# A graph layer on one core: first gathers taken from x, table B made before table A, lists and attributes loaded in pieces

## The chip, the core and the metric

The kernel runs on one core of a Trainium2 chip. Its engines work from queues of their own and meet through semaphores: TensorE (PE, with its weight loads shown apart as PEld), VectorE (DVE), ScalarE (ACT), GpSimd (POOL) and SyncE (SP), which here only issues transfers. The metric is the device time of one execution in microseconds, the median of several.

## The reference

A message-passing layer on a graph with N = 6250 nodes of H = 128 features and E = 100000 edges with 4 attributes each, all in float32. `dst` is sorted, `src` is not.

```python
msg_in = concatenate([x[src], x[dst], edge_attr], axis=1)      # E x 260
h = silu(msg_in @ mW1 + mb1)
messages = h @ mW2 + mb2
aggregated = segment_sum(messages, dst, num_segments=N)
u = silu(concatenate([x, aggregated], axis=1) @ uW1 + ub1)
updated = u @ uW2 + ub2
out = layernorm(x + layer_norm(x + updated, ln_g, ln_b))
```

## The kernel before, in words

Rather than multiply 260 features for each edge, the kernel first makes two tables of nodes in DRAM: `tab_a = x @ mW1[:128]` and `tab_b = x @ mW1[128:256] + mb1`. An edge's hidden row is then `tab_a[src] + tab_b[dst]` and the product of its four attributes, and after that the silu.

**Prologue.** `x` comes into `x_sb` (49 tiles of 128 nodes) by seven transfers, four on SP and three on ACT. Tiles go in groups of four: PE transposes them (L189), DVE copies the result to `xT` (L190), PE multiplies by the first part of `w1` (L196), ACT copies the product to `ta` (L198), SP stores it to `tab_a` (L199). When all of A is done the same `xT` is multiplied by the second part (L209), DVE adds the bias into `tb` (L211, three buffers) and SP stores it to `tab_b` (L212). Then come the four attribute rows of `mv` (L236); the attributes, which were loaded as one tile `ea_l` (L147), are turned on ACT in one copy (L242) and stored as four long rows `ea_d` (L243); and the lists of edges: `by_lane` (L123, and L128 for the last short group) brings `src_i` and `dst_i` so that a partition holds eight edges of each group, first for 14 groups, later for the other 84. `relative` (L223) forms the offset of each edge's `dst` from its group's first node, and L253 to L261 test that no group spans more than 96 nodes, for which a general path stands at the end. Last come the weights of the node update.

**Edges.** 98 groups of 1024 edges. For group g:

- `fetch` (L281): eight indirect transfers on POOL, each with 128 rows of `tab_a` by `src_i`, into a row buffer `ga`. There are seven buffers (AHEAD + 3).
- `load` (SP): 96 rows of `tab_b` from the group's first node into `mv` (L328), the attribute rows into `st` (L329), and `dst` of the group, broadcast to 96 partitions, into `near` (L334). It stands two groups ahead of the group that uses it.
- `matrices` (DVE): two one-hot matrices, `st` (node by edge, L341, from `near`) and `oh` (edge by node, L349, from `rel`).
- `hidden`: PE multiplies `st` by `mv` (L361, eight matmuls of two instructions each), which gives the B part and the attribute part at once; DVE adds the gathered rows into `s` (L363), after which the row buffer is free; ACT takes the silu into `h` (L365).
- `by_nodes`: PE multiplies `oh` by `h` (L372), ACT copies the sum to `sw` (L374).
- `add`: PE transposes `sw` (L379, L380) and DVE adds it to columns of `acc` and `deg` in SBUF (L383), at an address that is read from `base_i`.

The pools give `near`, `oh`, `s` and `sw` three buffers each, and PSUM two each for `pre`, `pw` and `pt`. SP's queue has the order of the code. On the other engines the scheduler of the language sets the order of work of neighbouring groups.

**Update.** In 13 groups of four tiles and then seven of seven, `acc` is multiplied by `mW2`, the update network is run, and the two layer norms are taken; the output goes out by SP.

Of the kernel before, what the change touches and what calls it, by code (L numbers as in the profile page):

```python
# [8 lines left out]
F32 = mybir.dt.float32  # L9
I32 = mybir.dt.int32  # L10
# [14 lines left out]
def kernel(  # L25
# [53 lines left out]
    LEAD = 2  # L79
    FIRST = 14  # L80
    XC = 8
    NM = 4
    assert NG % RB == 0
# [11 lines left out]


    prologue = ExitStack()
    prologue.enter_context(tc.manual_schedule(engines={ENG.SP}))
    x_sb = consts.tile([P, NT, H], F32, name="x_sb")
    nf = N // P  # L100
    w1 = consts.tile([P, 2, H], F32, name="w1")
    nc.scalar.dma_start(w1, mW1[: 2 * H].rearrange("(s k) f -> k s f", k=P))
    if N % P:
        nc.vector.memset(x_sb[:, nf, :], 0.0)
        nc.sync.dma_start(x_sb[: N - nf * P, nf, :], x[nf * P :])
    for k, (i0, n) in enumerate(groups(nf, XC)):
        eng = nc.sync if k % 2 else nc.scalar
        eng.dma_start(
            x_sb[:, i0 : i0 + n, :], x[i0 * P : (i0 + n) * P].rearrange("(i p) c -> p i c", p=P)
        )  # L110
# [21 lines left out]
    if rest:  # L132
        nc.vector.memset(src_i[:, full, :], 0)
        nc.vector.memset(dst_i[:, full, :], N)
    by_lane(src_i, src, 0, FIRST)
# [3 lines left out]
    by_lane(dst_i, dst, 0, FIRST)  # L139
    attrs = ExitStack()  # L140
    EQ = 80
    EJ = E // EQ
    assert E % EQ == 0
    ea_l = attrs.enter_context(tc.tile_pool(name="attrs", bufs=1, side="right")).tile(
        [EQ, EJ * ED], F32, name="ea_l"
    )
    nc.sync.dma_start(ea_l, edge_attr.rearrange("(q j) d -> q (j d)", q=EQ))  # L147
# [19 lines left out]
    nc.gpsimd.memset(acc, 0.0)  # L167
    deg = consts.tile([1, NW], F32, name="deg")
    nc.gpsimd.memset(deg, 0.0)
# [4 lines left out]
    ea_d = dram.tile([ED, NG * GE], F32, name="ea_d")  # L174
    xT = consts.tile([P, NP], F32, name="xT")
# [7 lines left out]
    with tc.tile_pool(name="tables", bufs=3) as work, tc.tile_pool(  # L183
        name="tables_ps", bufs=2, space=PSUM
    ) as ps:
        for i0, n in groups(NT, 4):
            pt = ps.tile([P, 4, P], F32, name="pt")
            for i in range(n):
                nc.tensor.transpose(pt[:, i, :], x_sb[:, i0 + i, :], ident)  # L189
            nc.vector.tensor_copy(  # L190
                xT[:, i0 * P : (i0 + n) * P], pt[:, :n, :].rearrange("p i f -> p (i f)")
            )
            pa = ps.tile([P, 4, H], F32, name="pa")
            for i in range(n):
                cols = slice((i0 + i) * P, (i0 + i + 1) * P)
                nc.tensor.matmul(pa[:, i, :], xT[:, cols], w1[:, 0, :], start=True, stop=True)  # L196
            ta = work.tile([P, 4, H], F32, name="ta")
            nc.scalar.copy(ta[:, :n], pa[:, :n])  # L198
            nc.sync.dma_start(by_node(tab_a)[:, i0 : i0 + n, :], ta[:, :n])  # L199

        b1 = bcast("b1", mb1)
        zeros = work.tile([W, H], F32, name="zeros")
        nc.vector.memset(zeros, 0.0)
        nc.sync.dma_start(tab_b[NP:NW], zeros)
        for i0, n in groups(NT, 4):
            pb = ps.tile([P, 4, H], F32, name="pa")
            for i in range(n):
                cols = slice((i0 + i) * P, (i0 + i + 1) * P)
                nc.tensor.matmul(pb[:, i, :], xT[:, cols], w1[:, 1, :], start=True, stop=True)  # L209
            tb = work.tile([P, 4, H], F32, name="tb")  # L210
            nc.vector.tensor_add(tb[:, :n], pb[:, :n], b1[:, None, :].to_broadcast([P, n, H]))  # L211
            nc.sync.dma_start(by_node(tab_b)[:, i0 : i0 + n, :], tb[:, :n])  # L212


        base_f = work.tile([1, NG], F32, name="base_f")
        nc.vector.tensor_copy(base_f, base_i)
        p_b = ps.tile([P, NG], F32, name="p_b")
        nc.tensor.matmul(p_b, ones[0:1, :], base_f, start=True, stop=True)
        nc.vector.tensor_copy(base_b, p_b)
        nc.vector.tensor_scalar(base_p, base_b, p_col, None, op0=OP.add)  # L220

# [8 lines left out]
    relative(0, FIRST)  # L230


    mv = []
    for k in range(NM):
        t = consts.tile([K1, H], F32, name=f"mv{k}")
        nc.sync.dma_start(t[W:], mW1[2 * H :])  # L236
        mv.append(t)
    with tc.tile_pool(name="lists", bufs=1) as work, tc.tile_pool(
        name="lists_ps", bufs=1, space=PSUM
    ) as ps:  # L240
        ea_t = work.tile([EQ, ED, EJ], F32, name="ea_t")
        nc.scalar.copy(ea_t, ea_l.rearrange("q (j d) -> q d j", d=ED))  # L242
        nc.sync.dma_start(ea_d[:, :E].rearrange("d (q j) -> q d j", q=EQ), ea_t)  # L243
        if E < NG * GE:
            pad = work.tile([ED, NG * GE - E], F32, name="pad")
            nc.vector.memset(pad, 0.0)
            nc.sync.dma_start(ea_d[:, E:], pad)
        by_lane(src_i, src, FIRST, NG)
        by_lane(dst_i, dst, FIRST, NG)
        relative(FIRST, NG)  # L250
        mid = (W - 1) / 2
        off = work.tile([P, NG, G], F32, name="off")
        nc.vector.tensor_scalar(off, rel, -mid, None, op0=OP.add)  # L253
        nc.vector.tensor_mul(off, off, off)
        far = work.tile([P, 1], F32, name="far")
        nc.vector.tensor_reduce(far, off.rearrange("p g i -> p (g i)"), AX.X, OP.max)
        pf = ps.tile([1, P], F32, name="pf")
        nc.tensor.transpose(pf, far, ident)  # L258
        farthest = work.tile([1, 1], F32, name="farthest")
        nc.vector.tensor_reduce(farthest, pf, AX.X, OP.max)  # L260
        nc.vector.tensor_scalar(bad_i, farthest, mid * mid, None, op0=OP.is_gt)  # L261
    attrs.close()
# [3 lines left out]
    nc.sync.dma_start(w2, mW2)  # L266
    u1 = consts.tile([P, 2, H], F32, name="u1")
    nc.sync.dma_start(u1, uW1.rearrange("(s k) f -> k s f", k=P))
    u2 = consts.tile([P, H], F32, name="u2")
    nc.sync.dma_start(u2, uW2)  # L270
    mb2_row = consts.tile([1, H], F32, name="mb2_row")
    nc.sync.dma_start(mb2_row, mb2.rearrange("(o f) -> o f", o=1))
    ub1_col = consts.tile([P, 1], F32, name="ub1_col")
    nc.sync.dma_start(ub1_col, ub1.rearrange("(f o) -> f o", o=1))
    ub2_b = bcast("ub2_b", ub2)
    g_b = bcast("g_b", ln_g)
    b_b = bcast("b_b", ln_b)
    prologue.close()

    def gather(t, tab, idx):  # L280
        nc.gpsimd.indirect_dma_start(  # L281
            out=t,
            out_offset=None,
            in_=tab[:, :],
            in_offset=bass.IndirectOffsetOnAxis(ap=idx, axis=0),
        )


    with ExitStack() as edges:
        held = edges.enter_context(tc.tile_pool(name="held", bufs=1))  # L290
        gath = edges.enter_context(tc.tile_pool(name="gath", bufs=AHEAD + 3))
# [14 lines left out]
        def fetch(g):  # L306
            if g >= NG:
                return
# [334 lines left out]
```

## Time and profile before

| | |
|---|---|
| median of 3 timed runs | 1445.85 us (1443.38 to 1451.78) |
| profiled execution | 1460.16 us, span 1458.3 us |
| busy share: PE, PEld, DVE, ACT, POOL | 56%, 50%, 27%, 14%, 58% |
| granted TensorE clock, mean over the span | 0.681 |
| DMA, mean over the span | 79 GB/s |

Times in the rows are in us from the start of the span. A timeline row gives start, length, engine, line, operation, what it writes and reads, how many instructions were merged (x), and in brackets the idle time of the engine just before and what ended it. "issue" there means that the profile shows nothing the engine waited for. A row of waits gives the total, the number and the longest. A row of stretches gives, for one stretch of time, the busy us and instruction counts of each engine, then the granted TensorE clock, the share of time in which the DMA engines were busy, and what they moved in GB/s.

### The profile page before, as it was taken

How to read it: one execution, taken by the hardware profiler on the slowest of the kernel's cores; microseconds unless marked ns; L12 is line 12 of the kernel's file. 1: busy time of each engine (PE TensorE's matmuls, PEld its weight loads, DVE VectorE, ACT ScalarE, POOL GpSimd, SP SyncE). 2: the span in 40 equal slices, each digit the busy share in tenths (PEclk: the TensorE clock that was granted, in tenths of full speed). 3: DMA queues.
4: the chain of work that ended last, by engine and by line, in shares of the span. 5: the costliest groups of instructions: out<-in, count | busy, mean ns of one | idle time of the engine just before them, and what ended most of it. 6: DMA issues, size and time to landing. Idle time of an engine off the chain costs nothing.

```text
span 1458.3 us, 11699 instructions
## 1 busy us (share of the span) xinstructions
PE 816.6 (56%) x3782; PEld 727.7 (50%) x3782; DVE 400.1 (27%) x803; ACT 197.9 (14%) x340; POOL 838.8 (58%) x814
## 2 busy tenths in 40 slices
PE   5410565837564673765726726756576647699700
PEld 5300455727453572655716726745465636594300
DVE  2101331313221231222303303323122212344543
ACT  1002110101110110111101101101011101112254
POOL 3670267657666766766667667666766666604110
PEclk9655566757656775667757757757665666689955
DMA  8424532323232332322323323322322222300011
GB/s 203 121 67 88 103 84 79 100 67 98 83 86 67 87 100 58 95 80 82 91 58 96 89 60 96 89 68 84 87 76 80 82 72 82 90 5 0 2 50 39
DMA packets 100906, 114.63 MB, mean 79 GB/s; under 512 B 42245, under 2 KB 78094, under 8 KB 100758
## 3 DMA queue, kind: packets, MB, share of 16 engines
q1 hardware_dynamic: 72358, 60.68, 14.8%
q0 software_dynamic: 25088, 51.43, 13.8%
q10 hardware_dynamic: 3392, 1.70, 0.5%
q8 instruction: 32, 0.52, 0.1%
q14 instruction: 36, 0.29, 0.1%
HBM read 102.47 MB, written 11.28 MB: 78 GB/s over the span
## 4 chain that ended last, share of the span: by engine, by line
PE 48%; issue 26%; another core or an unknown queue 14%; DVE 4%; ACT 4%; SPq 2%; DMA 1%; POOL 1%; DVEq 0%; ACTq 0%
PE pre L361 23%; PE pw L372 17%; ACT o L490 1%; ACT z L475 1%; SPq L128 1%; PE pa L196 1%; PE ps_y L437 1%; PE ps_a L423 1%; DVE s L363 1%; PE ps_u L427 1%; PE pt L380 1%; DVE st L416 1%; PE ps_u L428 1%; PE ps_a L422 1%
## 5 line engine op out<-in xcount | busy, mean ns | idle before, releaser
L281 POOL DMA_INDIRECT ga<-tab_a,src_i x784 | 797.1, 1017 | 464.9 <-issue 227.4
L361 PE MATMUL pre<-mv,st 100*128 100x128 f32 x1568 | 417.6, 415 | 145.2 <-issue 139.1
L361 PEld LDWEIGHTS pre<-mv,st 100*128 100x128 f32 x1568 | 392.5, 333 | 158.4 <-issue 157.3
L372 PE MATMUL pw<-h,oh 128*96 128x129 f32 x1568 | 301.2, 339 | 271.3 <-issue 266.2
L372 PEld LDWEIGHTS pw<-h,oh 128*96 128x96 f32 x1568 | 258.3, 213 | 310.4 <-issue 305.5
L363 DVE TENSOR_TENSOR s<-ga,pre 128x1024 f32<-128x1024 f32 x98 | 119.3, 1217 | 387.9 <-remote 222.1
L349 DVE TENSOR_TENSOR oh<-w_row,rel 128x768 f32<-128x768 f32 x98 | 93.2, 953 | 409.8 <-remote 322.2
L365 ACT ACTIVATE h<-s 128x1024 f32<-128x1024 f32 x98 | 103.7, 1058 | 629.4 <-DVE s L363 455.0
L374 ACT COPY sw<-pw 96x129 f32<-96x129 f32 x98 | 25.0, 255 | 390.6 <-remote 325.4
L341 DVE TENSOR_SCALAR st<-near,base_p 96x1024 f32<-96x1024 int32 x98 | 75.5, 770 | 4.9 <-DMA near<-in_dst_dram 2.7
L439 POOL TENSOR_TENSOR xu<-x_sb,ub_b 128x512 f32<-128x512 f32 (+1 forms) x13 | 15.6, 1204 | 73.1 <-PE pt L380 41.9
L209 PE MATMUL pa<-w,xT 128*128 128x128 f32 x98 | 19.9, 378 | 63.7 <-issue 38.5
L209 PEld LDWEIGHTS pa<-w,xT 128*128 128x128 f32 x98 | 17.9, 280 | 65.4 <-issue 39.3
L471 POOL TENSOR_TENSOR xb<-x_sb,b_b 128x896 f32<-128x896 f32 x7 | 14.5, 2075 | 48.2 <-DVE z L483 48.2
L383 DVE TENSOR_TENSOR acc<-acc,pt 128x96 f32 x98 | 24.2, 247 | 54.1 <-remote 47.1
L380 PE MATMUL pt<-ident,sw 96*1 96x96 f32 x98 | 26.6, 271 | 14.8 <-issue 14.8
L379 PE MATMUL pt<-ident,sw 96*128 96x96 f32 x98 | 27.3, 279 | 11.8 <-issue 11.6
L211 DVE TENSOR_TENSOR tb<-pa,b 128x512 f32<-128x512 f32 (+1 forms) x13 | 8.5, 660 | 75.8 <-remote 67.3
L379 PEld LDWEIGHTS pt<-ident,sw 96*128 96x128 f32 x98 | 16.6, 169 | 13.8 <-issue 13.3
L383 DVE TENSOR_TENSOR deg<-deg,pt 1x96 f32 x98 | 23.1, 235 | 0.6 <-DVE acc L383 0.6
L242 ACT COPY ea_t<-ea_l 80x5000 f32<-80x5000 f32 x1 | 9.0, 8979 | 85.8 <-DMA mv<-in_L_gnn_mW_dram 85.8
L258 PE MATMUL pf<-ident,far 128*1 128x128 f32 x1 | 0.4, 371 | 36.1 <-DMA b_b<-in_L_gnn_ln_b_dram 36.1
(70 smaller groups left out, 318.3 us busy)
## 6 DMA issues: line engine op xcount, KB each, us to landing
near<-in_dst_dram SPq DMA_DIRECT2D x97, 384.0 KB
ga<-tab_a,src_i POOLq DMA_INDIRECT x784
mv<-tab_b SPq DMA_DIRECT2D x98, 48.0 KB
tab_a<-ta SPq DMA_DIRECT2D x12, 256.0 KB
tab_b<-tb SPq DMA_DIRECT2D x12, 256.0 KB
out_dram<-o SPq DMA_DIRECT2D x6, 448.0 KB
st<-ea_d SPq DMA_DIRECT2D x98, 16.0 KB
ea_l<-in_edge_attr_dram SPq DMA_DIRECT2D x1, 1562.5 KB
```

The source lines that it names most:

```text
L209: nc.tensor.matmul(pb[:, i, :], xT[:, cols], w1[:, 1, :], start=True, stop=True)
L281: nc.gpsimd.indirect_dma_start(out=t, out_offset=None, in_=tab[:, :], in_offset=bass.IndirectOffsetOnAxis(ap=idx, axis=0),)
L341: nc.vector.tensor_scalar(stbuf[g % NST][:W], near.pop(g), base_p[:W, g : g + 1], None, op0=OP.is_equal,)
L349: nc.vector.tensor_tensor(oh, w_row[:, None, :].to_broadcast([P, G, W]), rel[:, g, :, None].to_broadcast([P, G, W]), op=OP.is_equal,)
L361: nc.tensor.matmul(pre[:, i, :], st[:, i, :], mv[g % NM], start=True, stop=True)
L363: nc.vector.tensor_add(s, rows.pop(g), pre)
L365: nc.scalar.activation(h[:, :, :H], s, AF.Silu)
L372: nc.tensor.matmul(pw, oh[:, i, :], h[:, i, :], start=i == 0, stop=i == G - 1)
L374: nc.scalar.copy(sw, pw)
L379: nc.tensor.transpose(pt[:, 0, :], sw[:, :H], ident[:W, :W])
L380: nc.tensor.transpose(pt[0:1, 1, :], sw[:, H:], ident[:W, :W])
L383: nc.vector.tensor_add(at, at, of)
```

## The change

- The first five groups (RAW) gather rows of `x` itself, which is an input, instead of rows of `tab_a`. Their product with the first part of `w1` is made in the edge stage: PE transposes the gathered rows into a `pre` buffer, DVE copies them to `xg`, and PE adds their product to the same PSUM tile as that of `st` and `mv`, so that the silu reads PSUM and no `s` is added. The list for these five groups is SP's first transfer, and the gathers are written ahead of the tables. `acc` and `deg` are zeroed on DVE instead of POOL.
- Transposes are followed by table B, and table A is made after it. Both go in groups of eight tiles. `xT` is now copied by ACT; two buffers `t` serve both tables. The PSUM buffers of the edge stage are used for the tables too (`pre` for products, `pt` through `narrow()` for everything small), and its pools are opened at the start.
- Lists come in five parts (5, 9, 28, 28 and 28 groups), the last three in the loop at groups 0, 2 and 4, followed by the comparison and the loads of the update's weights. Attributes come in ten pieces, nine of them in the loop, each eight groups ahead of its use.
- Row buffers go from seven to six (AHEAD + 2); `near`, `oh` and `s` from three to two; `load` brings `near` first.

```diff
+    RAW = 5
     FIRST = 14
-    XC = 8
+    LIST = 28
     NM = 4
...
+    edges = ExitStack()
+    edges.enter_context(tc.manual_schedule(engines={ENG.SP}))
+    held = edges.enter_context(tc.tile_pool(name="held", bufs=1))
+    gath = edges.enter_context(tc.tile_pool(name="gath", bufs=AHEAD + 2))
+    work = edges.enter_context(tc.tile_pool(name="edge", bufs=2))
+    ps = edges.enter_context(tc.tile_pool(name="edge_ps", bufs=2, space=PSUM))
...
+    by_lane(src_i, src, 0, RAW)
+    nc.scalar.dma_start(w1, mW1[: 2 * H].rearrange("(s k) f -> k s f", k=P))
...
-    nc.gpsimd.memset(acc, 0.0)
+    nc.vector.memset(acc, 0.0)
     deg = consts.tile([1, NW], F32, name="deg")
-    nc.gpsimd.memset(deg, 0.0)
+    nc.vector.memset(deg, 0.0)
...
+    def fetch(g):
+        if g >= NG:
+            return
+        rows[g] = gath.tile([P, G, H], F32, name="ga")
+        for i in range(G):
+            nc.gpsimd.indirect_dma_start(
+                out=rows[g][:, i, :],
+                out_offset=None,
+                in_=x if g < RAW else tab_a[:, :],
+                in_offset=bass.IndirectOffsetOnAxis(ap=src_i[:, g, i : i + 1], axis=0),
+            )
+
+    for g in range(RAW):
+        fetch(g)
...
+    def attributes(c):
+        t = turn.tile([EQ, EJ * ED], F32, name="ea_l")
+        chunk = edge_attr[c * EC : (c + 1) * EC]
+        nc.sync.dma_start(t, chunk.rearrange("(q j) d -> q (j d)", q=EQ))
+        ea_l[c] = t
+
+    def attribute_rows(c):
+        t = turn.tile([EQ, ED, EJ], F32, name="ea_t")
+        nc.scalar.copy(t, ea_l.pop(c).rearrange("q (j d) -> q d j", d=ED))
+        rows = ea_d[:, c * EC : (c + 1) * EC]
+        nc.sync.dma_start(rows.rearrange("d (q j) -> q d j", q=EQ), t)
...
+        def product(i0, n, part):
+            pm = ps.tile([P, G, H], F32, name="pre")
             for i in range(n):
                 cols = slice((i0 + i) * P, (i0 + i + 1) * P)
+                nc.tensor.matmul(pm[:, i, :], xT[:, cols], w1[:, part, :], start=True, stop=True)
+            return pm[:, :n]
+
+        for i0, n in groups(NT, G):
+            for k, m in groups(n, 4):
+                pt = narrow()
+                for i in range(m):
+                    nc.tensor.transpose(pt[:, i * P : (i + 1) * P], x_sb[:, i0 + k + i, :], ident)
+                nc.scalar.copy(xT[:, (i0 + k) * P : (i0 + k + m) * P], pt[:, : m * P])
+            pm = product(i0, n, 1)
+            tb = tables.tile([P, G, H], F32, name="t", bufs=2)
+            nc.vector.tensor_add(tb[:, :n], pm, b1[:, None, :].to_broadcast([P, n, H]))
+            nc.sync.dma_start(by_node(tab_b)[:, i0 : i0 + n, :], tb[:, :n])
...
+        attribute_rows(0)
+
+        for i0, n in groups(NT, G):
+            pm = product(i0, n, 0)
+            ta = tables.tile([P, G, H], F32, name="t", bufs=2)
+            nc.scalar.copy(ta[:, :n], pm)
             nc.sync.dma_start(by_node(tab_a)[:, i0 : i0 + n, :], ta[:, :n])
...
+        raw = g < RAW
+        if raw:
+            px = ps.tile([P, G, P], F32, name="pre")
             for i in range(G):
+                nc.tensor.transpose(px[:, i, :], ga[:, i, :], ident)
+            xg = work.tile([P, G, P], F32, name="s")
+            nc.vector.tensor_copy(xg, px)
+        pre = ps.tile([P, G, H], F32, name="pre")
+        st = stbuf[g % NST].rearrange("k (c i) -> k i c", i=G)
+        for i in range(G):
+            nc.tensor.matmul(pre[:, i, :], st[:, i, :], mv[g % NM], start=True, stop=not raw)
+            if raw:
+                nc.tensor.matmul(pre[:, i, :], xg[:, i, :], w1[:, 0, :], start=False, stop=True)
+        if raw:
+            nc.scalar.activation(h[:, :, :H], pre, AF.Silu)
             return h
...
+    for g in range(NG + 2):
+        if g % 2 == 0 and lists:
+            l0, l1 = lists.pop(0)
+            by_lane(src_i, src, l0, l1)
+            by_lane(dst_i, dst, l0, l1)
+            relative(l0, l1)
+            if l1 == NG:
+                compare()
+                weights()
+        for c in range(1, NC):
+            if g == max(1, c * EC // GE - 8):
+                attributes(c)
+            if g == max(1, c * EC // GE - 8) + 1:
+                attribute_rows(c)
+        if g + AHEAD >= RAW:
             fetch(g + AHEAD)
```

What POOL does from its last iota to the node update, before (`acc` and `deg` are the sums, `xu` is the update's):

```order
L157 IOTA p_col_i 128x1
L167 MEMSET acc 128x6368
L169 MEMSET deg 1x6368
L281 DMA ga<-tab_a,src_i 128x128 x784
L439 TENSOR_TENSOR xu<-x_sb,ub_b 128x512 x2
```

and after the change:

```order
L158 IOTA w_row_i 128x96
masks.py:199 AFFINE_SELECT ident<-ident 128x128
L162 IOTA p_col_i 128x1
L190 DMA ga<-in_x_dram,src_i 128x128 x40
L190 DMA ga<-tab_a,src_i 128x128 x744
```

The two memsets are gone, and the first forty of the 784 gathers read `x` and so wait for no table.

PE at the end of the tables and the start of the edges, before (`pa` holds products of either table, `pf` belongs to the comparison, `pre` and `pw` to the edges):

```order
L189 MATMUL pt<-ident,x_sb 128x128
L196 MATMUL pa<-w_63,xT 128x128
L209 MATMUL pa<-w_63,xT 128x128 x49
L258 MATMUL pf<-ident,far 1x128
L361 MATMUL pre<-mv_412,st_485 128x128 x8
L361 MATMUL pre<-mv_414,st_486 128x128 x8
```

and after the change (the row of 50 is the last tile of B and all 49 of A; `s` is here the buffer of `xg`):

```order
L262 MATMUL pt<-ident,x_sb 128x128
L273 MATMUL pt<-base_f,ones 128x98
L255 MATMUL pre<-w_79,xT 128x128 x50
L386 MATMUL pre<-ident,ga 128x128 x8
L392 MATMUL pre<-mv_94,st_449 128x128
L394 MATMUL pre<-w_79,s 128x128
L392 MATMUL pre<-mv_94,st_449 128x128
L394 MATMUL pre<-w_79,s 128x128
```

The comparison's transpose no longer stands between the tables and the edges, and the first group's matmuls are preceded by eight transposes of gathered rows and interleaved with their products.

More of the change, by code (lines that the diff above doesn't have):

```diff
@@ L181, in by_node, with narrow @@
         return t[:NP].rearrange("(i p) f -> p i f", p=P)
[L183 to L193, printed above, removed]
+    def narrow():
+        return ps.tile([P, 4 * P], F32, name="pt")
@@ L198 @@
[L198 to L212, printed above, removed]
@@ L228, in relative @@
         )
[L230 to L250, printed above, removed]
+    relative(0, RAW)
```

307 lines of the change are left out of this document (152 added, 155 removed).

## The prediction

> **What bounds the kernel now.** I read the page first, then the waits, then the timeline of POOL and PE, then stretches of it. From the page, the span, the busy shares and the costliest group:
>
> ```profile
> span 1458.3 us, 11699 instructions
> PE 816.6 (56%) x3782; PEld 727.7 (50%) x3782; DVE 400.1 (27%) x803; ACT 197.9 (14%) x340; POOL 838.8 (58%) x814
> L281 POOL DMA_INDIRECT ga<-tab_a,src_i x784 | 797.1, 1017 | 464.9 <-issue 227.4
> ```
>
> No engine is above 58%. The gathers on POOL are one unbroken list of 784, and their idle time is the thing to explain. The waits split it, and name the other loser:
>
> ```profile
> PEld pw L372 <- issue: 305.5, 208, 4.0
> POOL ga L281 <- issue: 227.4, 746, 0.3
> POOL ga L281 <- DVE s L363: 203.9, 25, 57.9
> ```
>
> The 0.3 us between two gathers belongs to them (0.94 + 0.30 = 1.25 us each, 10 us a group of eight). POOL waits 25 times for `s`, which frees a row buffer. Where in time, from POOL's timeline (start, length, engine, line, what):
>
> ```profile
> 42.24 1.11 POOL L281 DMA_INDIRECT ga<-tab_a,src_i  x1 [30.02 <-DMA tab_b<-zeros]
> 111.06 0.95 POOL L281 DMA_INDIRECT ga<-tab_a,src_i  x1 [0.30 <-issue]
> 169.94 1.21 POOL L281 DMA_INDIRECT ga<-tab_a,src_i  x1 [57.93 <-DVE s L363]
> 1273.32 0.94 POOL L281 DMA_INDIRECT ga<-tab_a,src_i  x1 [0.30 <-issue]
> 1316.16 2.48 POOL L439 TENSOR_TENSOR xu<-x_sb,ub_b 128x512 f32<-128x512 f32 x2 [41.89 <-PE pt L380]
> ```
>
> So the profiled span is four pieces: 42 us before any gather; seven groups gathered and then 58 us of standing still, to 169.9; 91 groups in 169.9 to 1273.3, 12.13 us each; and 185 us from the last gather to the end (43 of them the last edges on PE, the rest the node update). After 169.9 the 24 remaining stalls are 203.9 - 57.9 = 146 us, 6.1 us each and 1.6 us a group; the gathers themselves make 10.5. A run between stalls is 91/25 = 3.64 groups long.
>
> Why POOL stalls although PE is 56% busy is seen in PE's weight loads beside POOL's gathers, in stretches of time (length, then busy us and instructions of PE, PEld, DVE, ACT, POOL, granted clock, DMA share, GB/s), and at the seam between two of them:
>
> ```profile
> 60.00:112.00 52.00, 6.24 (x24) 5.35 (x24) 2.08 (x3) 0.00 (x0) 39.51 (x42) 0.50 0.26 68
> 119.00:123.00 4.00, 2.87 (x10) 2.28 (x10) 2.22 (x4) 0.00 (x0) 0.00 (x0) 0.50 0.31 89
> 185.00:204.00 19.00, 5.52 (x19) 3.23 (x19) 2.03 (x4) 0.26 (x1) 12.06 (x12) 0.54 0.17 45
> 204.00:235.00 31.00, 31.00 (x152) 31.00 (x151) 14.48 (x22) 6.12 (x9) 23.21 (x21) 0.78 0.44 116
> 185.62 0.35 PEld L372 LDWEIGHTS pw<-h,oh 128*96 128x96 f32 x3 [0.45 <-issue]
> 187.75 0.23 PEld L372 LDWEIGHTS pw<-h,oh 128*96 128x96 f32 x1 [1.78 <-issue]
> 199.73 0.94 POOL L281 DMA_INDIRECT ga<-tab_a,src_i  x1 [0.31 <-issue]
> 203.98 3.90 PEld L361 LDWEIGHTS pre<-mv,st 100*128 100x128 f32 x16 [0.64 <-issue]
> 205.68 1.71 POOL L281 DMA_INDIRECT ga<-tab_a,src_i  x1 [5.00 <-DVE s L363]
> ```
>
> PE falls into a crawl: one matmul in 1 to 2 us, waiting for nothing the profile names, while POOL gathers without a break. It starts 15 to 30 us after POOL's restart (169.9, then 185) and ends some 3 us after POOL has run out of buffers and stopped (200.7, then 204). Then PE does five times as much per us, frees a buffer, and POOL starts again. The whole edge stage is this cycle. The same crawl sits in the second half of the prologue, where the B table is made beside the first 56 gathers; it ends at 119, when they are through.
>
> **The change, part by part.** *First gathers.* The raw groups need `src` alone, not table A. Two memsets leave POOL, and the first list is SP's first transfer:
>
> ```profile
> 1.49 5.39 POOL L167 MEMSET acc<- 128x6368 f32 x1
> 6.83 5.39 POOL L169 MEMSET deg<- 1x6368 f32 x1
> 7.32 1.94 PE L189 MATMUL pt<-ident,x_sb 128*128 128x128 f32 x8 [7.32 <-DMA x_sb<-in_x_dram]
> ```
>
> A 512 KB load issued at 1.2 us has landed by 7.3, so a list of 20 KB lands at 3 to 7; take 5. Forty gathers at 1.25 us run from 5 to 55. On DVE the two memsets (at most what they took on POOL, 10.8 us) end by about 15, under the first transposes.
>
> *Tables.* B needs eight transposes and sixteen product instructions per eight tiles, as A did before; A alone needs products. Their pace before:
>
> ```profile
> 27.88 0.91 PEld L189 LDWEIGHTS pt<-ident,x_sb 128*128 128x128 f32 x8
> 31.21 0.91 PEld L189 LDWEIGHTS pt<-ident,x_sb 128*128 128x128 f32 x8
> 19.94 20.03 SPq L199 DMA_DIRECT2D tab_a<-ta  x13
> 44.01 7.66 PE L209 MATMUL pa<-w,xT 128*128 128x128 f32 x40 [3.02 <-DVE tb L211]
> ```
>
> 3.3 us per eight tiles with transposes; 7.66 us per 20 tiles without, 18.8 for all 49; 2.3 us from the last store's issue (39.97) to the first gather (42.24). Without the crawl B would stand at 8 + 20 = 28 and A at 49. But the gathers now run through this stage from 5 on. With the crawl from about 20 (15 us in, the early end; in the prologue of before it came after 9) some three of the six B groups are done; from 20 to 58 PE manages 38/1.7 = 22 of its instructions, one group more; then 2.2 groups x 3.3 = 7, A 17, landing 2.3: table A is there at **84 us** (75 if the crawl starts at 34, 95 if at 9). POOL stands from 55 to 84 and restarts with group 5. Before it restarted with group 7 at 169.9.
>
> *What stood between 119 and 164* goes from the path:
>
> ```profile
> 125.30 8.98 ACT L242 COPY ea_t<-ea_l 80x5000 f32<-80x5000 f32 x1 [85.80 <-DMA mv<-in_L_gnn_mW_dram]
> 136.19 10.46 SPq L128 DMA_DIRECT2D src_i<-in_src_dram  x1
> 147.13 5.24 SPq L128 DMA_DIRECT2D dst_i<-in_dst_dram  x1
> 155.06 0.86 DVE L223 TENSOR_TENSOR rel<-dst_i,base_b 128x672 f32<-128x672 int32 x1 [18.06 <-DMA dst_i<-in_dst_dram]
> ```
>
> The attribute copy (now 0.9 us ten times), the long lists, the comparison and the weights' loads move into the loop. They queue on SP ahead of `near`, `mv` and `st` of a group two ahead, and on ACT ahead of one `h`. I cost them at nothing: a group has 12 us and PE needs 6 of them. If that cover fails, see the last rival.
>
> *Raw groups.* Each adds 8 transposes, a copy of 128x1024 and 16 product instructions on PE, and drops one add. From these rows
>
> ```profile
> 29.43 1.86 PEld L196 LDWEIGHTS pa<-w,xT 128*128 128x128 f32 x16 [0.65 <-ACT ta L198]
> 28.62 1.29 DVE L190 COPY xT<-pt 128x512 f32<-128x512 f32 x2 [2.05 <-PE pt L189]
> 211.11 3.90 PEld L361 LDWEIGHTS pre<-mv,st 100*128 100x128 f32 x16
> 216.90 3.90 PEld L361 LDWEIGHTS pre<-mv,st 100*128 100x128 f32 x16
> ```
>
> an ordinary group takes PE 5.8 us when nothing hinders it; a raw one 5.8 + 0.9 + 1.9 (warm; twice that cold) + 1.3 for the copy it waits on, 10 to 12.7. That is as slow as POOL, so in these five groups the crawl is not caught up from slack: POOL stalls for a whole raw group, about 10 us, twice, where 1.6 a group is in the rate already. I add **10 us** (bounds 0 and 40, the latter five groups each 8 late).
>
> *Rate.* Row buffers go from seven to six, `near`, `oh`, `s` from three to two. While PE is fast it takes a group in 5.8 us and POOL brings one in 10.5, so in 20 us the ring drains by 1.5 groups. A ring of six isn't emptied by that either; run and stall stay. I keep 12.13 us (bounds 11.9 and 12.3). At the end the last backlog is up to one group shorter: 185 becomes 182.
>
> **Sum.** 84 + 93 x 12.13 (1128) + 10 + 182 = **1404 us** of span against 1458.3, 54 less. The profiled execution took 1460.16 us, its span 1458.3; the median of the three timed runs is 1445.85, 0.9% under it. Scaled, 1404 becomes **1392 us**, 3.7% faster. With the bounds of 84, 10 and the rate taken together, 1370 to 1430.
>
> **The rivals.** *No crawl in the tables.* If what slowed PE at 51 to 119 was something else, a cold clock or stores behind gathers, the tables are ready at 49 and POOL runs on from 55: 29 us earlier, 1375 of span, 1363 timed. For it: the clock was 0.50 there. Against it: at 119 to 123 the clock was 0.50 too and ten matmuls took 4 us, with no gather. 0.18. The Trainium skill (TensorE: Matmul & The Clock Gate, Part 1) has the array's clock halve after an idle window of about 3.4 us; by that rule alone PE would lose a factor of two in the tables, and this rival's time would hold. The trace does not bear it out as the cause: the rows of 119 and 60 have the same clock, and 2.5 against 0.5 matmuls per us.
>
> *The shorter ring shortens POOL's runs* (the slower side). If a ring of six takes a whole group off each run, 3.64 becomes 2.6, 93 groups make 36 runs and 35 stalls of 6.1, 213 us where 149 are in the rate: +64, span 1468, timed 1455, 0.7% slower than before. It decides from a run of 2.7 groups down. For it: POOL's stall is nothing but a full ring. Against it: the drain of 1.5 groups above. 0.10.
>
> *The pieces land on the path.* All that was moved into the loop, exposed: lists 16, attributes 9 x 1.1 of SP and 9 x 0.9 of ACT, comparison 4, weights 4: +42, span 1446, timed 1434. Against it: SP runs two groups ahead. 0.10. The Trainium skill (DMA: Bandwidth & Descriptors, Anatomy of one DMA) puts about 2.0 us of fixed cost on every DMA; 24 DMAs more (six for lists, eighteen for attributes) would by that be an estimated 48 us, if none were hidden, and the result 1440. No row here shows such a cost on the path: `near`, `mv` and `st` are three DMAs in each of 98 groups already.
>
> **How the numbers follow.** Forecast 0.62, the rivals 0.18, 0.10, 0.10. From the no-crawl case less its rate bound (1350) to the pieces' case (1440) leaves out the short ring and little more. A measurement of this kernel tells about 0.5% from no change, 7 us: under 1439 is faster. That is the forecast, the first rival and half of the third: 0.85; same, the other half, 0.05; slower 0.10.
>
> **What would show it.** First gather at 3 to 7 us, forty to 55; PE's product instructions slow between about 20 and 58; group 5's gather at 75 to 95; 24 to 27 stalls of about 6 us after it; last gather near 1222. A first `tab_a` gather under 60 is the first rival; 33 stalls or more the second; POOL stalls that end with a late `near` or `ea_t` the third. The forecast is wrong as a whole if the crawl behaves otherwise with six buffers or beside the raw groups.

## The result, and the profile after

The changed kernel takes 1391.15 us (median of 4 runs, 1378.75 to 1396.83) against 1444.62 us for the kernel before (1437.3 to 1451.78): a ratio of 0.9619, 95% interval 0.9535 to 0.9702. The profiled execution took 1396.83 us, its span is 1394.9 us, 63 us shorter than the span before.

From the page of the changed kernel, the span, the busy shares and the two groups of gathers, then from its waits those of POOL and the largest of PE:

```profile
span 1394.9 us, 11854 instructions
PE 834.0 (60%) x3902; PEld 746.2 (53%) x3902; DVE 400.9 (29%) x789; ACT 205.9 (15%) x356; POOL 817.8 (59%) x812
...
L190 POOL DMA_INDIRECT ga<-tab_a,src_i x744 | 748.8, 1006 | 421.3 <-issue 218.0
...
L190 POOL DMA_INDIRECT ga<-in_x_dram,src_i x40 | 38.0, 950 | 14.3 <-issue 11.9
```
```profile
PEld pw L407 <- issue: 236.0, 186, 5.6
POOL ga L190 <- issue: 229.8, 742, 1.6
POOL ga L190 <- DVE s L399: 151.2, 27, 10.7
POOL ga L190 <- DMA tab_a<-t: 42.2, 1, 42.2
```

The 58 us for which POOL stood before is now one wait of 42.2 us for table A, and the other stalls for a row buffer are much as they were: 27 of 5.6 us, where there were 24 of 6.1. Where these lie, from POOL's timeline:

```profile
3.98 1.12 POOL L190 DMA_INDIRECT ga<-in_x_dram,src_i  x1 [2.44 <-DMA src_i<-in_src_dram]
96.06 0.94 POOL L190 DMA_INDIRECT ga<-tab_a,src_i  x1 [42.18 <-DMA tab_a<-t]
1223.02 0.95 POOL L190 DMA_INDIRECT ga<-tab_a,src_i  x1 [0.30 <-issue]
```

So the span is now 96.1 us to group 5's gather, 93 groups in 1127.0 us (12.12 each), and 171.9 us from the last gather's start to the end. Against before, group 5 stands where group 7 stood, 74 us earlier.

What the tables look like beside the raw gathers is seen in the rows of PE's weight loads, DVE and ACT on both sides of one gap, and in stretches of time (the columns as before: PE, PEld, DVE, ACT, POOL, clock, DMA share, GB/s):

```profile
24.88 1.64 PEld L262 LDWEIGHTS pt<-ident,x_sb 128*128 128x128 f32 x8
60.75 3.36 PEld L255 LDWEIGHTS pre<-w,xT 128*128 128x128 f32 x16 [34.23 <-ACT xT L263]
17.75 1.23 DVE L266 TENSOR_TENSOR t<-pre,b 128x1024 f32<-128x1024 f32 x1 [3.03 <-issue]
53.79 1.23 DVE L266 TENSOR_TENSOR t<-pre,b 128x1024 f32<-128x1024 f32 x1 [34.81 <-remote]
60.12 1.07 ACT L263 COPY xT<-pt 128x512 f32<-128x512 f32 x2 [38.17 <-remote]
```
```profile
30.00:54.00 24.00, 0.00 (x0) 0.00 (x0) 0.21 (x1) 0.00 (x0) 18.08 (x20) 0.50 0.20 52
60.00:76.00 16.00, 14.16 (x101) 12.96 (x102) 5.80 (x10) 4.56 (x9) 0.00 (x0) 0.88 0.35 100
```

PE issued the second product and the next transposes by 26.5 us. DVE's addition to that product begins at 53.8, just as POOL's fortieth gather ends, and ACT's copy of those transposes at 60.1. In the 24 us from 30 to 54 POOL gathered 20 times and PE, ACT and DVE did next to nothing. "remote" in brackets means that the profile cannot name what ended the wait. This is the slow stretch that the prediction called a crawl, in a harder form: not one matmul in 1 to 2 us but none, and DVE and ACT stand with PE.

The packed trace holds more than the views show, and it says what came late. DVE and ACT wait here for updates of PE's semaphore. The product that DVE adds to ended at 25.3 us (matmul ends are modelled), and its update stands in the trace at 53.76; the first transposes that ACT copies ended at 26.15, and theirs stands at 60.09. Either engine starts 0.03 us after its update. From 64 to 90 us, when no gather runs, each update follows its matmul by 0.01 to 0.02 us. Records of semaphore updates, landings of transfers among them, are also missing: the trace holds 6029, where a complete one of the same program (chip F below) holds 19121; for the kernel before it is 6338 and 18894. So "issue" and "remote" in the result's two traces can stand for a wait whose record is missing, and the prediction's "waiting for nothing the profile names" says less than it seems to.

### The profile page after: what moved, and what is told of

Same layout as the page of the kernel before. It is cut to its first block, busy times and chain, and to the rows that moved or that the text cites. A ratio compares the mean times of both kernels' runs of the same rounds, so it can differ in the third digit from the quotient of the medians.

```text
span 1394.9 us, 11854 instructions
## 1 busy us (share of the span) xinstructions
PE 834.0 (60%) x3902; PEld 746.2 (53%) x3902; DVE 400.9 (29%) x789; ACT 205.9 (15%) x356; POOL 817.8 (59%) x812
## 3 DMA queue, kind: packets, MB, share of 16 engines
q0 software_dynamic: 25088, 51.43, 14.8%
## 4 chain that ended last, share of the span: by engine, by line
PE 40%; another core or an unknown queue 22%; issue 20%; DVE 5%; ACT 5%; POOL 4%; DMA 2%; DVEq 1%; SPq 0%; POOLq 0%; ACTq 0%
PE pre L392 18%; PE pw L407 14%; POOL ga L190 4%; DVE s L399 2%; ACT o L539 1%; ACT z L524 1%; ACT h L400 1%; PE ps_y L486 1%; PE ps_a L472 1%; PE ps_u L476 1%; DVE st L465 1%; PE pre L394 1%; PE ps_u L477 1%; PE ps_a L471 1%
## 5 line engine op out<-in xcount | busy, mean ns | idle before, releaser
L190 POOL DMA_INDIRECT ga<-tab_a,src_i x744 | 748.8, 1006 | 421.3 <-issue 218.0
L407 PE MATMUL pw<-h,oh 128*96 128x129 f32 x1568 | 311.3, 349 | 232.4 <-issue 204.2
L407 PEld LDWEIGHTS pw<-h,oh 128*96 128x96 f32 x1568 | 268.7, 221 | 269.8 <-issue 236.0
L399 DVE TENSOR_TENSOR s<-ga,pre 128x1024 f32<-128x1024 f32 x93 | 113.3, 1219 | 356.5 <-issue 148.6
L400 ACT ACTIVATE h<-s 128x1024 f32<-128x1024 f32 x93 | 98.3, 1057 | 527.0 <-DVE s L399 319.6
L255 PE MATMUL pre<-w,xT 128*128 128x128 f32 x196 | 29.2, 312 | 44.7 <-ACT xT L263 34.5
L255 PEld LDWEIGHTS pre<-w,xT 128*128 128x128 f32 x196 | 27.2, 223 | 46.7 <-ACT xT L263 35.4
L190 POOL DMA_INDIRECT ga<-in_x_dram,src_i x40 | 38.0, 950 | 14.3 <-issue 11.9
L394 PE MATMUL pre<-w,s 128*128 128x128 f32 x80 | 21.0, 355 | 8.5 <-DVE s L388 8.0
L266 DVE TENSOR_TENSOR t<-pre,b 128x1024 f32<-128x1024 f32 (+1 forms) x7 | 7.6, 1092 | 52.5 <-remote 34.8
```

The lines of the kernel that those rows point to most:

```text
L190: nc.gpsimd.indirect_dma_start(out=rows[g][:, i, :], out_offset=None, in_=x if g < RAW else tab_a[:, :], in_offset=bass.IndirectOffsetOnAx ...
L255: nc.tensor.matmul(pm[:, i, :], xT[:, cols], w1[:, part, :], start=True, stop=True)
L394: nc.tensor.matmul(pre[:, i, :], xg[:, i, :], w1[:, 0, :], start=False, stop=True)
L399: nc.vector.tensor_add(s, ga, pre)
L400: nc.scalar.activation(h[:, :, :H], s, AF.Silu)
L407: nc.tensor.matmul(pw, oh[:, i, :], h[:, i, :], start=i == 0, stop=i == G - 1)
```

## The experiments

Twelve runs were made in four sittings; those of one sitting ran on one chip, beside runs of the kernel before. Where they ran mattered more than most of the edits. In the first, second and fourth sitting the kernel before took 1214.7, 1214.0 and 1213.2 us (two chips, **F** below); in the third, on another chip, it took 1443.9, much as in the result (1444.6). The record does not name the result's chip; **S** below means either. S was met in one sitting only besides the result, so chip and moment are not told apart there. The comparisons below are between ratios to the kernel before, or between times on chips F, where the kernel before took the same within 0.2% each time.

**Both kernels again (chips F).** Unaltered copies.

> The changed kernel once more, unaltered, since in the first sitting of experiments the kernel before took 1214.7 us where it had taken 1444.6, and the two times cannot be set side by side. Theory (there PE does not fall into its slow stretches, POOL's gathers run without a stall and alone set the end): on a chip that behaves so, 784 gathers of about 1.31 us begin at 4 us, the gap between the raw gathers and table A is about 5 us and the last gather lies near 1040; span 1185 to 1195, ratio 0.975 to 0.985. On a chip with the slow stretches: 0.955 to 0.970 again. Rival (something else in the new loop costs time where the slow stretches are gone): ratio 0.99 or more.

> The kernel before, unaltered, for its profile in this sitting. Theory: where PE has no slow stretches, POOL gathers seven groups from 42 us, stands until the first edges free a row buffer after the lists and attributes, some 20 to 40 us, and then never stalls again: 91 groups of 10.5 us, span 1205 to 1225, and the B table done by about 65 us in place of 119. Where it has them: B at 119, 25 stalls, span 1435 to 1460.

> The changed kernel unaltered, beside the next two on the same chip. On a chip with PE's slow stretches (before near 1444): ratio 0.955 to 0.970, as in the first sitting. On one without them (before near 1214): 0.980 to 0.987, as in the run called again.

Measured: the changed kernel 1196.35 us, ratio 0.9837 (0.9806 to 0.9869), and on the other chip 1193.57 us, 0.9827 (0.9784 to 0.9869); the kernel before 1213.58 in its one profiled run, span 1211.8. First and last gather from POOL's timeline, and two stretches, of the kernel before on chip F:

```profile
42.21 1.11 POOL L281 DMA_INDIRECT ga<-tab_a,src_i  x1 [29.98 <-DMA b<-in_L_gnn_mb_dram]
...
1058.32 0.95 POOL L281 DMA_INDIRECT ga<-tab_a,src_i  x1 [0.30 <-issue]
```
```profile
40.00:60.00 20.00, 12.24 (x92) 10.74 (x91) 8.49 (x13) 0.00 (x0) 13.53 (x15) 1.00 0.75 209
400.00:600.00 200.00, 151.67 (x655) 146.36 (x656) 61.55 (x100) 24.19 (x40) 152.77 (x156) 0.67 0.37 96
```

and of the changed kernel there (span 1194.0), with two of its waits:

```profile
4.08 1.11 POOL L190 DMA_INDIRECT ga<-in_x_dram,src_i  x1 [2.54 <-DMA src_i<-in_src_dram]
61.28 0.94 POOL L190 DMA_INDIRECT ga<-tab_a,src_i  x1 [4.46 <-DMA tab_a<-t]
1039.46 0.94 POOL L190 DMA_INDIRECT ga<-tab_a,src_i  x1 [0.30 <-issue]
```
```profile
30.00:54.00 24.00, 20.45 (x165) 18.72 (x165) 7.63 (x13) 7.36 (x11) 18.82 (x18) 1.00 0.82 229
```
```profile
DVE s L399 <- DMA ga<-tab_a,src_i: 559.2, 77, 10.3
...
POOL ga L190 <- DMA tab_a<-t: 4.5, 1, 4.5
```

The row 30 to 54 is the same program in the same stretch as the row of zeros above: 165 weight loads and 18 gathers here, none and 20 there. On F no gather ever waits for a row buffer, in either kernel (the lists of waits have no such line), DVE waits for gathers instead, and POOL's list sets the end. There the gain of 17.8 us adds up: the first gather 38.1 earlier, the 784 gathers 19.3 longer from first to last (4.5 of them the wait for table A; the rest is a mean gather of 1.012 us in place of 0.993), the tail 1.1 longer. The expectation for the kernel before had a stand of 20 to 40 us after seven groups on F; there was none.

**No raw gathers (chip F).** RAW = 0, and the first gathers stand behind the tables:

```diff
-    RAW = 5
+    RAW = 0
...
-    relative(0, RAW)
     relative(RAW, FIRST)
+    for g in range(AHEAD):
+        fetch(g)
```

> The changed kernel with RAW = 0: no gather runs beside the tables, B is still made ahead of A, all 98 groups are gathered from table A. Theory (the gathers are what slows PE in the tables): with no gather there, six B steps of 3.3 us and an A stage of some 17 us end near 50 us, first gather 48 to 60, PE's product instructions back to back in the tables. From there 98 groups at 12.1 us, less some 13 us because the first ring fills without a stall: last gather about 1225 as in the changed kernel, time 1385 to 1405. Rival (the tables are slow for a reason of their own, cold clock or two t buffers): table A still comes at 93 us, the first gather at 96, and five groups more are to be gathered after it: 1445 to 1455.

Measured: 1237.39 us, ratio 1.0186 (1.0164 to 1.0208), 41 us over the changed kernel on that chip. POOL's first and last gather:

```profile
59.07 1.12 POOL L190 DMA_INDIRECT ga<-tab_a,src_i  x1 [57.54 <-DMA tab_a<-t]
1083.86 0.94 POOL L190 DMA_INDIRECT ga<-tab_a,src_i  x1 [0.30 <-issue]
```

Table A is there at 59.1 us without a gather beside it, and at 61.3 with forty. So on F the gathers cost the tables 2 us, and gathering raw rows is worth all of the change's gain there: without them the new order is slower than the kernel before, whose A comes first, at 42. The theory's "first gather 48 to 60" holds; its 1385 to 1405 was written for chip S, where this kernel was not run.

**Five row buffers (chip F).** `bufs=AHEAD + 2` to `bufs=AHEAD + 1`.

> The changed kernel with five row buffers in place of six (AHEAD + 1). Theory of the prediction: the ring is not what ends PE's slow stretch, runs and stalls stay; per group 12.1 us, time 1380 to 1402. Rival (one buffer fewer takes up to one group off each of POOL's runs): about nine stalls of 6 us more, 1440 to 1455. Third reading (PE turns slow only when POOL is some five groups ahead of the edges, as it was at the onsets in both kernels; with five buffers POOL stops before that): the slow stretches are shorter or gone, per group under 11.8 us, time under 1370.

Measured: 1193.31 us, ratio 0.9828 (0.9805 to 0.985), the same as the changed kernel's. But where no gather waits for a buffer the run cannot tell the three readings apart: the one question it was made for stayed open, until the result itself is read for it (below).

**The pieces back ahead of the loop (chip F).** Lists, comparison, weights and nine attribute pieces:

```diff
+    for l0, l1 in lists:
+        by_lane(src_i, src, l0, l1)
+        by_lane(dst_i, dst, l0, l1)
+        relative(l0, l1)
+    compare()
+    weights()
+    for c in range(1, NC):
+        attributes(c)
+        attribute_rows(c)
     for g in range(LEAD):
         load(g)
...
```

> The changed kernel with the moved pieces put back ahead of the loop: lists 14 to 98, the comparison, the weights' loads and attribute pieces 1 to 9. Theory (they were on the path before and are hidden in the loop): the first edge group starts 30 to 45 us later, POOL waits for it with a full ring, time 1420 to 1435. Rival (in the loop they cost what they cost ahead of it): no change, 1380 to 1402.

Measured: 1246.56 us, ratio 1.0266 (1.0246 to 1.0285), 50 us over the changed kernel. POOL's stall, and the first and last attribute copies moved:

```profile
131.13 0.94 POOL L190 DMA_INDIRECT ga<-tab_a,src_i  x1 [50.82 <-PE pre L386]
81.69 1.07 ACT L213 COPY ea_t<-ea_l 80x500 f32<-80x500 f32 x1 [23.87 <-DMA ea_l<-in_edge_attr_dram]
117.08 1.07 ACT L213 COPY ea_t<-ea_l 80x500 f32<-80x500 f32 x1 [3.52 <-DMA ea_l<-in_edge_attr_dram]
```

On the path they cost 50 us, 4.4 of it for each attribute piece (a load, a copy of 1.07 us and a store, one after the other in one buffer). In the loop of the changed kernel one wait of 2.1 us is put down to them. The mechanism holds on F; the price on the path was put at 42. On S the run was not made.

**Table A ahead of B (chip F).** The two product loops change places; DVE copies A, and B's bias is added in the second.

> The changed kernel with table A made before B; the raw gathers stay. Table A is then ready near 78 us and group 5's gather starts there, 18 us before the changed kernel's 96. Theory (the first edges need both tables, and a ring of six holds the five raw groups and one more): POOL stops again after one group until the first raw group is through, so nothing is won: 1380 to 1402. Rival (the restart of POOL alone sets the end): 18 us less, 1365 to 1380.

Measured: 1183.36 us, ratio 0.9734 (0.9706 to 0.9762), about 1% better than the changed kernel. The 784 gathers run from 3.96 to 1034.58 us without one stall; the wait of 4.5 us for table A is gone too. Neither expectation was right as to size on F: with the first edges soon enough the ring does not fill, so the earlier table counts, but there were only 5 to 13 us to win. On S this order ran only together with `st` on ScalarE (below). There POOL waited 16 us less for table A than in the result (25.8 against 42.2) and 17 us more for row buffers (168.6 against 151.2), and the time stayed level, which is what the theory says, though two edits were made at once.

**Gathers replaced by plain transfers (chip S).** On top of A first; one transfer of 1024 consecutive rows a group, from POOL too. The rows that come are then not those of the edges:

```diff
-        for i in range(G):
-            nc.gpsimd.indirect_dma_start(
...
+        tab = x if g < RAW else tab_a
+        k = (g % 6) * GE
+        nc.gpsimd.dma_start(rows[g], tab[k : k + GE, :].rearrange("(p i) f -> p i f", i=G))
```

> Table A made before B, and each group's eight gathers replaced by one plain transfer of 1024 consecutive rows, issued from POOL as well: the indices are left out, bytes and buffers are the same. It shows what the rest of the kernel takes when the gathers cost POOL next to nothing. Theory: PE is next, 5.8 to 7 us a group, start near 80 us, tail 150: 800 to 920 in all; and PE runs without slow stretches on any chip, since no gather is under way. Rival (the transfers themselves, or a chain through DVE and ScalarE, bind the group): 1000 or more. Rival for the first sitting's slow stretches (they come from something other than the gathers): on a chip that has them they stay, time over 1200.

Measured, in one run: 858.25 us where the kernel before took 1443.87. Its span, two stretches, and POOL's largest wait:

```profile
span 856.1 us, 10788 instructions
```
```profile
30.00:54.00 24.00, 21.33 (x165) 19.51 (x163) 12.86 (x21) 5.94 (x10) 0.53 (x1) 0.95 0.66 185
400.00:600.00 200.00, 196.73 (x1044) 194.04 (x1043) 96.31 (x154) 43.13 (x66) 16.42 (x31) 0.88 0.52 155
```
```profile
POOL ga L191 <- DVE s L395: 522.3, 87, 12.6
```

The same bytes go into the same buffers, on a chip that has the slow stretches, and the slow stretches are gone: 165 matmuls in the stretch from 30 to 54, PE busy for 98% of 400 to 600. So on S the other engines stand still beside the indirect gathers and not beside the traffic as such. The edit changes two things at once, though: the kind of the transfers, and their number (98 for 784, in 14112 packets for 25088). Many small plain transfers were not tried. Together with F, where the same gathers do no harm, the gathers as they are issued here are necessary and not sufficient, and what differs on S stays open.

Two other causes can be looked for in the traces. Loads of instructions do not end the standing in the tables: in the result's trace none moved between the start and 68.7 us. The profiler's own recording can't be ruled out as the cause: records are missing where the engines stand, and they are all there in this run on S (4776 records of landings of SP's and ACT's transfers; 1927 in the result, 4761 in the changed kernel on F). Every run on record comes with a span and a granted clock, and so with a recording; none shows whether the recording holds the engines, or the same thing holds up engines, signals and records. A packet of the gather queue takes as long on S as on F (0.13 us, from 14.8% of 16 engines over 1394.9 us for 25088 packets on S and 17.2% over 1194.0 on F).

**st as a tensor_tensor (chip F).** On F a gather is the bound, and once a group one takes some 1.5 us in place of 0.95. With A first, `st` from `near` and a broadcast `base_p`:

```diff
-        nc.vector.tensor_scalar(
+        nc.vector.tensor_tensor(
             stbuf[g % NST][:W],
             near.pop(g),
-            base_p[:W, g : g + 1],
-            None,
-            op0=OP.is_equal,
+            base_p[:W, g : g + 1].to_broadcast([W, GE]),
+            op=OP.is_equal,
         )
```

> Table A made before B (as in the run of that name), and st, the comparison of near with base_p, is written as a tensor_tensor with base_p broadcast in place of a tensor_scalar with a scalar per partition: the same values. Theory (a gather is lengthened from 0.95 to about 1.5 us, once a group, by the st that runs beside it, because DVE's fast form shuts POOL out; the broadcast form runs at one element a cycle and does not): st grows from 0.74 to about 1.1 us, the lengthened gathers are nearly gone, and where POOL sets the end the time falls by up to 52 us against the table A first version, to about 1135. Rival (any DVE operation with its operands in SBUF shuts POOL out): the gathers beside st grow by 1.1 us, time about 30 us longer. Where PE has its slow stretches, the theory expects little: under 15 us.

Measured: 1217.75 us, ratio 1.0028 (1.0008 to 1.0048): 34 us slower than A first alone. The theory fell, and about the rival's 30 us came.

**st on ScalarE (chips S and F).** With A first, `st` is made in two activations on ScalarE, and `base_p` is negated for them:

```diff
-        nc.vector.tensor_scalar(base_p, base_b, p_col, None, op0=OP.add)
+        nc.vector.tensor_scalar(base_p, base_b, p_col, -1.0, op0=OP.add, op1=OP.mult)
...
+        st = stbuf[g % NST][:W]
+        nc.scalar.activation(st, near.pop(g), AF.Abs, bias=base_p[:W, g : g + 1])
+        nc.scalar.activation(st, st, AF.Relu, bias=ones[:W, 0:1], scale=-1.0)
```

> Table A made before B, and st made on ScalarE, as relu(1 - |near - (base + p)|) in two activations of 96x1024, in place of one comparison on DVE: the same zeros and ones. Theory (what lengthens a gather is a DVE operation with all its operands in SBUF that runs beside it; with st off DVE only oh is left): the gathers over 1.2 us fall from 86 to under 45, their mean busy time from 1.011 to under 0.97 us, and where POOL sets the end the time falls 25 to 50 us below the table A first version, to 1135 to 1160; ScalarE gains 2.1 us a group, which lies beside the gathers. Rival (the lengthening has another source, or ScalarE's part comes onto the path before h): 1180 or more. On a chip where PE has its slow stretches: within 15 us of the table A first version's share of before, since POOL stands 200 us there in any case.

> The version with st on ScalarE and table A first, once more, because the first time it met a chip with the slow stretches. Theory: there it is level with the changed kernel (within 1%), since POOL stands over 200 us waiting for buffers whatever a gather costs; on a chip without them the lengthened gathers are gone from the path and it takes 1135 to 1165, ratio to before 0.935 to 0.960. Rival: 1180 or more there, ratio above 0.97.

Measured on F: 1155.44 us, ratio 0.9528 (0.9485 to 0.9571), the fastest of all; on S: 1389.24 us, 0.9611 (0.9557 to 0.9665), level with the changed kernel's 0.9619. The group of table gathers in A first, in the tensor_tensor version and in this one on F, one row from each page:

```profile
L190 POOL DMA_INDIRECT ga<-tab_a,src_i x744 | 753.6, 1013 | 226.7 <-issue 218.7
```
```profile
L190 POOL DMA_INDIRECT ga<-tab_a,src_i x744 | 785.3, 1055 | 226.7 <-issue 220.0
```
```profile
L190 POOL DMA_INDIRECT ga<-tab_a,src_i x744 | 716.5, 963 | 230.1 <-issue 218.5
```

The mean gather goes from 1.013 us to 1.055 when `st` lasts 1.21 us in place of 0.74, and to 0.963 when it leaves DVE; over 744 gathers that is +32 and -37 us, and the times moved by +34 and -28 (these are three sittings; by the ratios +36 and -25). In A first 86 gathers of 784 take over 1.2 us, 63 of them mostly beside `st` and 22 mostly beside `oh`; with `st` on ScalarE 25 do, all beside `oh`. So the theory held on F. The Trainium skill (SBUF — State Buffer, Who interferes with whom) has DVE and GpSimd share one pair of ports, held for a whole instruction by a DVE operation in a two-port mode or, against a GpSimd operation that reads SBUF, by one with two SBUF inputs; whoever comes second waits. By that rule both forms of `st` hold up a gather, which reads its indices from SBUF, and ScalarE's does not: the three rows agree. On S the same version buys nothing over the changed kernel, as expected, since POOL stands there for row buffers in any case (168.6 us in 29 waits), although its mean gather fell to 0.981 us there too.

**A break after each group (chip F).** A POOL copy of one column of the group's last row block, meant to wait until the gathers have landed:

```diff
+        nc.gpsimd.tensor_copy(landed, rows[g][:, G - 1, 0:1])
```

> Table A made before B, and POOL waits after each group's eight gathers until they have landed (it copies one column of the last row block), 1.5 to 2.5 us of standing still in every 12. On a chip without slow stretches this only costs: 98 x about 1.8 us, 1350 to 1390. On a chip with them there are two theories. One (PE and the others stop when gathers have been under way without a break for 15 us or more, so a break each 10 us prevents it): B and A are done near 62 us, no slow stretch in the loop, 1350 to 1390, the same as on the other chip. Other (it is the share of time in which gathers are under way that counts, breaks or not): the engines stand in the tables until the fortieth gather, near 65 us, stalls for row buffers stay, 1400 to 1480.

Measured: 1226.87 us. The copy was ordered four gathers behind the group that it reads, so it waited 12 times in 98 (25.5 us in all) and there was no break of the kind meant; and the chip was F. It tells nothing of the slow stretches, and whether breaks prevent them was not tried otherwise.

## Why the prediction was right, step by step

The sum came to 1404 us of span, and 1394.9 was measured. Three terms were off: table A by +12 us, rate and raw groups by -11, the tail by -10. Two of them paid for the third, so that the time came within 1 us of 1392 is luck; the four pieces of the span and the way they moved were foreseen.

- **First gathers, 5 and 55 us.** 3.98, and the fortieth ends at 53.9.
- **Table A, 84 us (75 to 95).** 96.06, just past the bound. Two steps failed. "Some three of the six B groups are done" by 20 us: one was, on S and on F. ACT's copy of the first attribute piece stands ahead of the copies of `xT` that PE needs, and waits for its load. PE's wait on S, and ACT's on F, where it is named:

```profile
21.52 3.78 PE L255 MATMUL pre<-w,xT 128*128 128x128 f32 x16 [7.34 <-issue]
```
```profile
19.78 1.07 ACT L213 COPY ea_t<-ea_l 80x500 f32<-80x500 f32 x1 [9.08 <-DMA ea_l<-in_edge_attr_dram]
```

  These 7 us have no term in the sum, which had the pieces at nothing. And "from 20 to 58 PE manages 38/1.7 = 22 of its instructions": it managed none from 30 to 54, so that two steps of B were done when PE came back and not four. (Its own row, 24 instructions in 52 us, gives 2.2 us for one and not 1.7.) B then took 15 us from 60 at the pace foreseen (the stretch 60 to 76), and A 18, held by its two `t` buffers:

```profile
78.47 1.93 ACT L281 COPY t<-pre 128x1024 f32<-128x1024 f32 x2 [4.31 <-DMA tab_b<-t]
79.51 13.53 SPq L282 DMA_DIRECT2D tab_a<-t  x7
```

- **Raw groups, +10 (0 to 40), and the rate, 12.13.** Together (1128 + 10)/93 = 12.24 us a group; 12.12 was measured with the raw groups in it. The extra was at its lower bound, 0: between 96 and 160 us POOL stalls three times, for 1.8 to 3.0 us, where two stalls of some 10 us were foreseen.
- **Tail, 182.** 171.9. Before, six groups were still to be added after the last gather, and the last `s` began 37.5 us after it (1310.8); now five, and 25.3 us (1248.3). Behind that the update takes the same 147 us. The term of one group, 3 us, should have been 12. The backlog is worked off by PE, at 5.8 us a group or more, and before, PE's last slow stretch went on until 4.4 us after the last gather (weight loads one by one until 1277.7), which it hardly did after.
- **The pieces, nothing.** Right for those in the loop, as far as the waits show it; the first piece, ahead of the loop, cost the 7 us above. The run with the pieces put back prices what was removed at 50 us on F, not 42. No run prices one of the 24 transfers alone; one after the other, an attribute piece with its two transfers and its copy took 4.4 us.
- **The ring, no change.** Right on S, by the result alone: 12.12 us a group with six buffers (the raw groups among them) and 12.13 with seven, 27 stalls of 5.6 us and not 35 of 6.1. The second rival is out there.
- **The first rival** (no crawl in the tables, table A at 49 and a time of 1363) took a cold clock for the cause. On S it is out: at a granted clock of 0.50 PE could not come to nothing for 24 us. On F, where there is no slow stretch, table A came at 61 us and not 49: its price was 12 us too low for its own case, 7 of them the wait for the first attribute piece. The rule that stands beside it (the Trainium skill, TensorE: Matmul & The Clock Gate, Part 1) makes a factor of two; the row of zeros is more than that, and by that rule the clock of 0.50 in that row follows from PE's idleness.

The account of the crawl was half right. On S it goes with the gathers: plain transfers in their place end it. But the prediction spoke of it as the nature of these gathers, and chips F have none of it with the same instructions; and that PE waits "for nothing" was read from a trace that lacks two thirds of the records of semaphore updates. The 3.8% is a number of S; on F the same change brings 1.6 to 1.7%, by another sum, in which the 38 us of earlier gathers are the only gain and 20 us go back to longer gathers, a gap and the tail. What each part of the change is worth on S was read from the two traces alone; the runs that take a part out were made on F.

## What to carry to other kernels

Before an edge of a few per cent is explained from one trace, see the same two kernels on a second chip: here the bound itself (buffers behind slow stretches, or POOL's list) changed between sittings on different chips, and with it what an edit is worth. Where a list of indirect gathers sets the end, start it from an input instead of a product, and try the work that DVE does in SBUF beside it on another engine: ScalarE did the same comparison for some 25 us less. Before an engine is said to wait "for nothing", count the records of semaphore updates in the trace against a run that has them all. Then replace the suspect's instructions, with bytes and buffers left alone, and change the kind and the number of transfers in two runs and not in one.

## What was not expected of the hardware

- One program, 1444 to 1445 us in two sittings and 1213 to 1215 us in three on two other chips, with mean granted clocks of 0.68 and 0.71 and the same packets. In the first, PE, DVE and ACT come to a stop, for 24 us and more at a time, while POOL issues indirect gathers one after another (0 weight loads in 30 to 54 us against 165), and go on within 6.3 us of POOL's stop. Updates of PE's semaphore stand 28.5 and 33.9 us behind the matmuls that make them, and two thirds of the trace's records of semaphore updates, landings of transfers among them, are missing. No run shows why.
- A gather of 128 rows of 512 bytes occupies POOL for 0.94 us and 0.30 between two; beside `st` and `oh` on DVE it takes up to 2.0 us (A first, chip F). Taking `st` off DVE brought the mean from 1.013 to 0.963.
- Without indirect gathers the kernel is bound by PE, 6.5 us a group (1044 matmuls in 200 us, 34 a group), and takes 858 us: on S some 38% of the changed kernel's time hangs on the way rows are fetched.
